# Masks of relation 0 on GpSimd instead of VectorE, with other distances in a written timetable

## The chip, the cores and the metric

The kernel runs on one core of a Trainium2 chip. A core has a matrix engine (TensorE, "PE" in the profile, with its weight loads as "PEld"), VectorE ("DVE"), ScalarE ("ACT"), GpSimd ("POOL") and SyncE ("SP"), which here issues all DMA transfers. The metric is the device time of one execution in microseconds (us), as the median of several runs. TensorE writes its results into PSUM[...].

## The reference, cut to what matters

128 graphs of 128 nodes with 256 features pass through two layers, all in float32.

- Layer 0 is two graph attention steps (GAT): `Wh = h W`, a score for each pair of nodes from two vectors, leaky ReLU, scores where there is no edge replaced by a very low number, softmax, and the weighted sum of `Wh`. Then a residual, a layer norm, a feed-forward (256 to 1024 to 256, ReLU), a residual and a layer norm.
- Layer 1 is an attention of 8 heads with 4 relations, then a layer norm, a feed-forward with GELU, a layer norm. Its core is

```
attn = softmax(q k^T / sqrt(dh))
for r in range(4):
    v_r = src @ Wv[r] + bv[r]
    out += (attn * (adj == r)) @ v_r
```

The change is about `attn * (adj == r)`. The adjacency holds the integers 0 and 1, but the kernel computes all four relations, as the reference does.

## The kernel before, in words

The graphs are worked on in 32 groups of G = 4. Each group goes through five stages, written as Python generators: load, GAT (`gat_block`, with `gat_weighting` called twice), the feed-forward of layer 0 (`feed_forward`), `attention`, and the feed-forward of layer 1. Several groups are in flight at once, one in each stage or two.

The order of the work is set by a timetable. Every `yield TIMES[...]` in a stage says how much later its next piece is due. A heap (`todo`, lines 587 to 613) always takes the piece with the earliest due time, at the same time the earlier stage first. Group g's stages start at 100 g plus -75, -39, 48, 132 and 300, except at the first and last groups, where `EARLY` shifts them. TensorE and SyncE must keep the order in which the pieces are taken (`KEPT`; TensorE from due time 250 on). On VectorE, ScalarE and GpSimd a planner puts the instructions in order by its own estimate of when they are ready. Each engine then works through its list strictly in that order, and waits are semaphores.

The lines that the change and the steps of the prediction touch:

- GAT: L392 computes `wh` and L393 copies it. In `gat_weighting` a row of scores is turned by L366 and sent through DRAM (`zs`, `zsd`), L373 is the leaky ReLU, L374 applies `cap` (made by L387 from the adjacency, `at`), L376 the maximum, L379 the exponential, L381 on GpSimd the division. L400 and L410 are the two weighted sums on TensorE, and L401 copies L400's result.
- Feed-forward: seven products of half size for each unit (L307; a fast matrix scheme), with two units in turn. L313, L314, L320 copy, L321, L322, L325 add on VectorE, L327 and L333 are the activations on ScalarE. The last product of each unit adds to the PSUM tile `chain`, and must come after L325 has read that tile. L350 is the second matrix, L351 the residual. L283 to L286 on GpSimd make the sums of the inputs that the products use.
- Attention: L424 and L430 give q and k, L435 copies the adjacency into PSUM as float32 (`adj`), L444 the scores of one graph (`weights`), L450 the maximum, L454 the exponential, L456 on GpSimd the division, then `turned` transposes the weights (L262 and a round trip through DRAM, `zd`, into `eT`). L470 makes the four masked copies `m` of `eT`, one for each relation, L477 and L478 give `v` for all relations, L489 the weighted sum of all relations and heads (64 instructions for a graph, relation 3 first and 0 last in each half), L493 copies it, L527 applies `Wo`.
- Layer norms: L230 and L231 on VectorE, L233 to L237 on GpSimd, L239 on ScalarE; the gains and offsets that are still to be applied are L245 on GpSimd (`affine`).
- `mm`, the tile for nearly all results of TensorE, has six PSUM buffers; `adj` and `av` have one each.

Of the kernel before, what the change touches and what calls it, by code (L numbers as in the profile page):

```python
# [12 lines left out]
F32 = mybir.dt.float32  # L13
I32 = mybir.dt.int32
AF = mybir.ActivationFunctionType
OP = mybir.AluOpType
# [6 lines left out]
P = 128  # L23
G = 4

TIMES = {
    "sums": 5, "ff unit": 3, "ff2": 4, "ff half": 10, "row": 13, "gat": 16, "wh": 5.5,
    "gat copy": 2, "qk": 4.5, "scores": 5.5, "turn0": 10, "turn1": 5,
    "v0": 5.5, "mask0": 0, "av": 6.5, "v": 3.5, "mask": 3,
    "end": 1, "lead ff0": 26, "lead att": 32, "lead ff1": 32, "affine": 7,  # L30
    "store": 25,
# [26 lines left out]
def graph_layers(ctx: ExitStack, tc: tile.TileContext, a: dict, out: bass.AP):  # L58
# [8 lines left out]
    nc = tc.nc  # L67
    x, xT, adjT = a["x"], a["xT"], a["adjT"]
    NG, N, _, D = x.shape
# [6 lines left out]
    R = a["wv"].shape[1] // D  # L76
    H = 8
# [7 lines left out]
    wk = ctx.enter_context(tc.tile_pool(name="wk", bufs=2))  # L85
# [14 lines left out]
    def load_mask(g):  # L100
        at = ld.tile([P, G, N], I32, name="at")
        nc.sync.dma_start(at, adjT[g])
        return at

    def wload(name, t=None):

        k, m = a[name].shape
        if t is None:
            t = cst.tile([P, k // P, m], F32, name=name)
        nc.sync.dma_start(t, a[name].rearrange("(c p) m -> p c m", p=P))  # L110
        return t
# [11 lines left out]
    m = wload("M", wk.tile([P, DC, MW], F32, name="m_in", tag="wh", bufs=1))  # L123
# [100 lines left out]
    def normalised(y, first=0, n=G):  # L224

        y = y[:, first:first + n]
        mv = sm.tile([P, n, 2], F32, name="mv")
        for b in range(n):
            st = sm.tile([P, 6], F32, name="st")
            nc.vector.bn_stats(st, y[:, b])  # L230
            nc.vector.bn_aggr(mv[:, b], st)  # L231
        rstd = sm.tile([P, n], F32, name="rstd")
        nc.gpsimd.tensor_scalar(rstd, mv[:, :, 1], EPS, None, op0=OP.add)  # L233
        nmr = sm.tile([P, n], F32, name="nmr")
        nc.gpsimd.tensor_scalar(nmr, mv[:, :, 0], -1.0, None, op0=OP.mult)
        nc.gpsimd.tensor_tensor(rstd, rstd, mhalf[:, :n], OP.pow)
        nc.gpsimd.tensor_mul(nmr, nmr, rstd)  # L237
        for b in range(n):
            nc.scalar.activation(y[:, b], y[:, b], AF.Identity, bias=nmr[:, b:b + 1], scale=rstd[:, b:b + 1])  # L239
# [117 lines left out]
    def gat_weighting(wh, c, cap, direct):  # L357

        e = wk.tile([P, G, N], F32, name="e")
        if direct:  # L360
            p = ps.tile([P, G, N], F32, name="mm")
            for b in range(G):
                nc.tensor.transpose(p[:, b], wh[:, b, c + 1:c + 2].to_broadcast([P, N]), ident)
        else:
            z = sm.tile([P, G, Q], F32, name="zs", bufs=2)
            nc.vector.transpose(z, wh[:, :, c + 1:c + 2].to_broadcast([P, G, Q]))  # L366
            s = dr.tile([G, NQ, Q], F32, name="zsd")
            nc.sync.dma_start(s.rearrange("b i t -> i b t"), z[::Q])
            p = e
            nc.sync.dma_start(p, bass.AP(tensor=s.tensor, offset=s.offset, ap=[[0, P], [1, G * N]]))  # L370
        yield TIMES["row"]
        for b in range(G):
            nc.scalar.activation(e[:, b], p[:, b], AF.Prelu, bias=wh[:, b, c:c + 1], alpha=ALPHA)  # L373
        nc.vector.scalar_tensor_tensor(e, cap, BIG, e, op0=OP.subtract, op1=OP.min)  # L374
        nm = sm.tile([P, G], F32, name="nm")
        nc.vector.tensor_reduce(nm, e, AX.X, OP.max, negate=True)  # L376
        s = sm.tile([P, G], F32, name="s")
        for b in range(G):
            nc.scalar.activation(e[:, b], e[:, b], AF.Exp, bias=nm[:, b:b + 1], accum_out=s[:, b:b + 1])  # L379
        nc.vector.reciprocal(s, s)  # L380
        nc.gpsimd.tensor_mul(e, e, per_row(s, N))  # L381
        return e

    def gat_block(direct, tag, g, xt, at):

        cap = wk.tile([P, G, N], F32, name="cap")
        nc.vector.tensor_scalar(cap, at, 0, 2 * BIG, op0=OP.is_gt, op1=OP.mult)  # L387
        wh = wk.tile([P, G, MW], F32, name="wh", tag=tag, bufs=TB if tag == "T" else 1)
        for b in range(G):
            p = ps.tile([P, MW], F32, name="mm")  # L390
            for c in range(DC):
                nc.tensor.matmul(p, xt[:, c, ts(b, N)], wx[:, c], start=c == 0, stop=c == DC - 1)  # L392
            nc.scalar.copy(wh[:, b], p)  # L393
            if b % 2:
                yield TIMES["wh"]
        att = yield from gat_weighting(wh, D + 2, cap, direct)
        yield TIMES["gat"]
        for b in range(G):
            p = ps.tile([P, D + 2], F32, name="mm")
            nc.tensor.matmul(p, att[:, b], wh[:, b, :D + 2], start=True, stop=True)  # L400
            nc.scalar.copy(wh[:, b, :D + 2], p)  # L401
        yield TIMES["gat copy"]
        y = wk.tile([P, G, D], F32, name="tok", bufs=KB)
        nc.sync.dma_start(y, x[g])
        att = yield from gat_weighting(wh, D, cap, direct)
        yield TIMES["gat"]
        for b2_ in range(0, G, 2):
            p = ps.tile([P, 2, D], F32, name="mm")
            for b in (b2_, b2_ + 1):
                nc.tensor.matmul(p[:, b - b2_], att[:, b], wh[:, b, :D], start=True, stop=True)  # L410
            nc.vector.tensor_add(y[:, b2_:b2_ + 2], y[:, b2_:b2_ + 2], p)
        normalised(y)
        return y

    def attention(y, g, first, direct):

        hT = features(y, first or direct)
        at = load_mask(g)
# [14 lines left out]

        adj = ps.tile([P, G, N], F32, name="adj", bufs=1)
        nc.vector.tensor_copy(adj, at)  # L435

        def weights(b):


            scores = [ps.tile([P, DC, 2, N], F32, name="mm") for _ in range(2)]  # L440
            for c in range(DC):
                for h in range(2):
                    rows = ts(h, P // 2)
                    nc.tensor.matmul(scores[h][:, c], qT[rows, c, ts(b, N)], kbd[c][rows, b],  # L444
                                     start=True, stop=True, tile_position=(h * P // 2, 0))
            e = wk.tile([P, H, N], F32, name="e1")
            for h, p in enumerate(scores):
                p = p.rearrange("p c q n -> p (c q) n")
                nm = sm.tile([P, HC], F32, name="nm1")
                nc.vector.tensor_reduce(nm, p, AX.X, OP.max, negate=True)  # L450
                s = sm.tile([P, HC], F32, name="s1")
                eh = e[:, ts(h, HC)]
                for q in range(HC):
                    nc.scalar.activation(eh[:, q], p[:, q], AF.Exp, bias=nm[:, q:q + 1], accum_out=s[:, q:q + 1])  # L454
                nc.vector.reciprocal(s, s)  # L455
                nc.gpsimd.tensor_mul(eh, eh, per_row(s, N))  # L456
            return e

        def turned(e):
            eT = wk.tile([P, H, N], F32, name="eT")  # L460
            transposed(e, eT, direct, e)
            return eT

        def by_relation(b, eT, ms, parts):


            ab = adj[:, b][:, None, :].to_broadcast([P, H, N])
            for r in parts:
                m = ms[r] = wk.tile([P, H, N], F32, name="m", bufs=R)
                nc.vector.scalar_tensor_tensor(m, ab, r, eT, op0=OP.is_equal, op1=OP.mult)  # L470

        def values(b):
            v = wk.tile([P, R, D], F32, name="v")
            for r in range(0, R, 2):
                p = ps.tile([P, 2, D], F32, name="mm")
                for f in range(DC):
                    nc.tensor.matmul(p, hT[:, b, f], wv[:, f, r:r + 2], start=f == 0, stop=f == DC - 1)  # L477
                nc.vector.tensor_add(v[:, r:r + 2].rearrange("p r d -> p (r d)"),  # L478
                                     p.rearrange("p r d -> p (r d)"), bv[:, r * D:(r + 2) * D])
            return v  # L480
# [20 lines left out]
        eT = [turned(es[0])]  # L501
        yield TIMES["turn1"]
        eT.append(turned(es[1]))
        yield TIMES["v0"]
        PARTS = range(R)
        v, ms = values(0), {}
        for k in range(0, 8, 2):
            by_relation(0, eT[0], ms, PARTS[k // 2:k // 2 + 1])
            yield TIMES["mask0"]
        for b in range(G):  # L510
# [8 lines left out]
            for k in range(0, 8, 2):  # L519
                if b + 1 < G:  # L520
                    by_relation(b + 1, eT[b + 1], ms, PARTS[k // 2:k // 2 + 1])
                if k == 2 and b + 1 < G:
# [30 lines left out]
    def stage_gat(g):  # L553
        x0[g] = yield from gat_block(g < 2, "T" if g == 1 else "wh", g, *loads.pop(g))
# [109 lines left out]
```

## Time and profile before

| | |
|---|---|
| median of 3 runs | 3208.48 us (3208.29 to 3210.35) |
| span of the profiled execution | 3208.9 us |
| TensorE busy | 3124.8 us, 97% |
| VectorE busy | 2019.9 us, 63% |
| ScalarE busy | 1688.2 us, 53% |
| GpSimd busy | 1377.3 us, 43% |
| masks, L470 on VectorE | 512 operations, 598.8 us |
| DMA | 320.8 MB, 43.5% of 16 engines |

A group of instructions in the profile is named by line, engine and operation, with what it writes and reads. "Idle before" is the time that the engine stood still just ahead of an instruction, with the instruction on another engine that released it. In the timeline, consecutive instructions of one kind are one row, with their number. A float32 matmul of the program is two matmul instructions in the trace.

### The profile page before, as it was taken

Reading aid. Unit: us, or ns where it says so; the run is one execution under the profiler, and the core shown is the slowest. Engines: PE = TensorE matmul, PEld = TensorE weight load, DVE = VectorE, ACT = ScalarE, POOL = GpSimd, SP = SyncE. Lnnn points to the kernel's source line nnn. Section 1 sums busy time; section 2 is a strip of 40 time slices with the busy share of each in tenths; the row PEclk is TensorE's granted clock in tenths of the full one; section 3 lists DMA queues with packets and bytes.
Section 4 is the critical chain, followed back from the end, with each engine's and each line's share of the span. In section 5 each row is a group of like instructions: output and inputs, shape, how many; then the busy total and the mean of one; then the engine's idle time right before and its main releaser. Section 6 shows DMA issues by size and latency. Waiting matters only on the chain.

```text
span 3208.9 us, 55180 instructions
## 1 busy us (share of the span) xinstructions
PE 3124.8 (97%) x20160; PEld 2377.2 (74%) x20160; DVE 2019.9 (63%) x3654; ACT 1688.2 (53%) x5063; POOL 1377.3 (43%) x1734
## 2 busy tenths in 40 slices
PE   6989999999999999999999999999999999999998
PEld 5756777777777777777777777777777777777666
DVE  3566566666566666576666576666576666576563
ACT  4435555555555555555555555555555555555443
POOL 2324345345345344345344345344345344345342
PEclk8999999999999999999999999999999999999999
DMA  4244454444454444454444454444454444454310
GB/s 156 66 105 96 102 119 102 107 99 100 102 120 104 105 98 101 101 120 104 105 100 98 101 120 104 104 99 99 102 120 104 104 99 99 102 120 92 73 34 14
DMA packets 1156399, 320.82 MB, mean 100 GB/s; under 512 B 902944, under 2 KB 1126688, under 8 KB 1156000
## 3 DMA queue, kind: packets, MB, share of 16 engines
q1 hardware_dynamic: 1156128, 317.29, 43.5%
q8 instruction: 160, 2.62, 0.3%
q14 instruction: 111, 0.91, 0.1%
HBM read 187.58 MB, written 129.62 MB: 99 GB/s over the span
## 4 chain that ended last, share of the span: by engine, by line
PE 58%; DVE 4%; DMA 1%; issue 0%; ACT 0%; POOL 0%; SPq 0%; ACTq 0%; POOLq 0%; DVEq 0%
PE mm L350 18%; PE mm L307 15%; PE mm L477 7%; PE av L489 5%; DVE m L470 3%; PE mm L444 3%; PE mm L527 2%; PE mm L430 2%; PE mm L424 2%; PE mm L392 2%; PE mm L400 1%; PE mm L410 1%; DVE fT L325 0%; DVE fT L322 0%; DMA eT<-zd 0%
## 5 line engine op out<-in xcount | busy, mean ns | idle before, releaser
L470 DVE SCALAR_TENSOR_TENSOR m<-adj,eT 128x1024 f32<-128x1024 f32 x512 | 598.8, 1213 | 242.5 <-DMA eT<-zd 176.9
L245 POOL TENSOR_TENSOR tok<-tok,ln_rows 128x512 f32<-128x512 f32 (+1 forms) x636 | 668.6, 1059 | 42.2 <-PE mm L256 14.8
L456 POOL TENSOR_TENSOR e<-e,s 128x512 f32<-128x512 f32 x256 | 266.1, 1040 | 660.9 <-DVE s L455 648.9
L454 ACT ACTIVATE e<-mm,nm 128x128 f32<-128x128 f32 x1024 | 359.8, 374 | 199.7 <-DVE nm L450 178.0
L477 PE MATMUL mm<-wv,T 128*128 128x512 f32 x1024 | 464.2, 596 | 0.0
L350 PE MATMUL mm<-wf,fT 128*128 128x256 f32 x2048 | 456.9, 381 | 0.0
L350 PE MATMUL mm<-w,fT 128*128 128x256 f32 x2048 | 455.5, 381 | 1.1 <-DVE v L478 1.1
L350 PEld LDWEIGHTS mm<-w,fT 128*128 128x128 f32 x2048 | 386.6, 190 | 75.5 <-issue 23.8
L350 PEld LDWEIGHTS mm<-wf,fT 128*128 128x128 f32 x2048 | 386.4, 190 | 63.3 <-ACT wh L401 8.9
L239 ACT ACTIVATE tok<-tok,nmr,rstd 128x256 f32<-128x256 f32 x512 | 269.2, 594 | 137.7 <-POOL nmr L237 125.1
L477 PEld LDWEIGHTS mm<-wv,T 128*128 128x128 f32 x1024 | 191.5, 190 | 199.6 <-issue 189.3
L351 DVE TENSOR_TENSOR tok<-tok,mm 128x512 f32<-128x512 f32 x128 | 87.8, 686 | 299.4 <-PE mm L350 295.4
L381 POOL TENSOR_TENSOR e<-e,s 128x512 f32<-128x512 f32 x64 | 66.9, 1046 | 475.3 <-DVE s L380 381.1
L489 PE MATMUL av<-m,v 128*32 128x128 f32 x8192 | 256.2, 277 | 8.1 <-DVE v L478 4.2
L489 PEld LDWEIGHTS av<-m,v 128*32 128x32 f32 x8192 | 219.8, 111 | 54.1 <-issue 42.2
L283 POOL TENSOR_TENSOR t<-T 128x256 f32<-128x256 f32 x64 | 46.7, 729 | 483.6 <-DMA T<-zd 483.6
L454 ACT ACTIVATION_READ_ACCUMULATOR e<-mm,nm 128x1 f32 x1024 | 218.8, 214 | 0.0
L450 DVE TENSOR_REDUCE nm<-mm 128x4 f32<-128x512 f32 x256 | 162.9, 676 | 64.0 <-PE mm L444 64.0
L478 DVE TENSOR_TENSOR v<-mm,bv 128x512 f32<-128x512 f32 x256 | 167.5, 684 | 46.9 <-PE mm L477 46.9
L307 PE MATMUL mm<-T,w 128*128 128x256 f32 x768 | 196.5, 385 | 0.2 <-ACT T L260 0.2
L307 PE MATMUL mm<-T,wf 128*128 128x256 f32 x768 | 192.6, 380 | 0.0
L373 ACT ACTIVATE e<-e,wh 128x128 f32<-128x128 f32 x240 | 77.3, 408 | 210.2 <-DMA e<-zsd 210.2
(123 smaller groups left out, 5090.1 us busy)
## 6 DMA issues: line engine op xcount, KB each, us to landing
zd<-e SPq DMA_DIRECT2D x496, 128.0 KB, 3.1
eT<-zd SPq DMA_DIRECT2D x124, 512.0 KB, 4.0
zd<-T SPq DMA_DIRECT2D x364, 128.0 KB, 4.0
T<-zd SPq DMA_DIRECT2D x91, 512.0 KB, 4.0
xt<-in_xT_dram SPq DMA_DIRECT2D x32, 512.0 KB
at<-in_adjT_dram SPq DMA_DIRECT2D x64, 256.0 KB, 6.2
tok<-in_x_dram SPq DMA_DIRECT2D x32, 512.0 KB
out_dram<-tok SPq DMA_DIRECT2D x31, 512.0 KB, 7.5
```

The costliest lines, as they stand in the source:

```text
L239: nc.scalar.activation(y[:, b], y[:, b], AF.Identity, bias=nmr[:, b:b + 1], scale=rstd[:, b:b + 1])
L245: engine.tensor_tensor(y[:, b:b + n], y[:, b:b + n], v[:, None, :].to_broadcast([P, n, D]), op)
L307: nc.tensor.matmul(p[:, i], win[k][:, ts(f0 + i, P)], hs[k], start=first and i == 0, stop=True, skip_group_check=True)
L350: nc.tensor.matmul(p[:, b - b2_], fT[f][:, ts(b, N)], wout[:, f], start=n == 0, stop=n == FC - 1)
L444: nc.tensor.matmul(scores[h][:, c], qT[rows, c, ts(b, N)], kbd[c][rows, b], start=True, stop=True, tile_position=(h * P // 2, 0))
L450: nc.vector.tensor_reduce(nm, p, AX.X, OP.max, negate=True)
L454: nc.scalar.activation(eh[:, q], p[:, q], AF.Exp, bias=nm[:, q:q + 1], accum_out=s[:, q:q + 1])
L456: nc.gpsimd.tensor_mul(eh, eh, per_row(s, N))
L470: nc.vector.scalar_tensor_tensor(m, ab, r, eT, op0=OP.is_equal, op1=OP.mult)
L477: nc.tensor.matmul(p, hT[:, b, f], wv[:, f, r:r + 2], start=f == 0, stop=f == DC - 1)
L478: nc.vector.tensor_add(v[:, r:r + 2].rearrange("p r d -> p (r d)"), p.rearrange("p r d -> p (r d)"), bv[:, r * D:(r + 2) * D])
L489: last = nc.tensor.matmul(po[ts(q, DH), c], v[:, r, c * P + q * DH:c * P + (q + 1) * DH], ms[r][:, q // 2 * HC + c * 2 + q % 2], start=r = ...
```

## The change

```diff
 TIMES = {
-    "sums": 5, "ff unit": 3, "ff2": 4, "ff half": 10, "row": 13, "gat": 16, "wh": 5.5,
-    "gat copy": 2, "qk": 4.5, "scores": 5.5, "turn0": 10, "turn1": 5,
+    "sums": 6, "ff unit": 3, "ff2": 5, "ff half": 10, "row": 13, "gat": 18, "wh": 7.5,
+    "gat copy": 3, "qk": 4.5, "scores": 6, "turn0": 10, "turn1": 5,
...
-        cap = wk.tile([P, G, N], F32, name="cap")
+        cap = wk.tile([P, G, N], F32, name="cap", bufs=1)
...
         nc.vector.tensor_copy(adj, at)
+        zero = wk.tile([P, G, N], F32, name="zero", bufs=1)
+        nc.vector.tensor_scalar(zero, at, 0, None, op0=OP.is_equal)
...
-                nc.vector.scalar_tensor_tensor(m, ab, r, eT, op0=OP.is_equal, op1=OP.mult)
+                if r == 0:
+                    nc.gpsimd.tensor_mul(m, eT, zero[:, b][:, None, :].to_broadcast([P, H, N]))
+                else:
+                    nc.vector.scalar_tensor_tensor(m, ab, r, eT, op0=OP.is_equal, op1=OP.mult)
...
-        PARTS = range(R)
+        PARTS = (0, 3, 2, 1)
```

Of the four masked copies of each graph's weights, the one of relation 0 is now made by GpSimd: VectorE writes once for each group a tile `zero` with 1 where the adjacency is 0 and 0 elsewhere, and GpSimd multiplies. It is meant to take work from VectorE and give it to the less busy GpSimd. The copies are asked for in the order 0, 3, 2, 1, so that GpSimd's is asked for first and VectorE makes them in the order in which L489 reads them. `cap` has one buffer instead of two, which makes room in SBUF for `zero`. The timetable gives GAT, the feed-forwards and the scores other distances, so that the stages of neighbouring groups are interleaved in another order on TensorE.

## The prediction

> **What bounds the kernel now.** I read four views in this order: the busy totals, the busy time by stretch, the waits of TensorE alone, and then the timeline of one period, first TensorE, then VectorE and ScalarE beside it.
>
> ```profile
> PE 3124.8 (97%) x20160; PEld 2377.2 (74%) x20160; DVE 2019.9 (63%) x3654; ACT 1688.2 (53%) x5063; POOL 1377.3 (43%) x1734
> ```
> TensorE is busy for all but 84 us; no other engine comes near. By stretch (columns: span, then busy time of PE, PEld, DVE, ACT, POOL, granted clock, DMA):
> ```profile
> 300.00:2900.00 2600.00, 2583.78 (x16853) 1971.10 (x16853) 1688.55 (x3051) 1420.87 (x4271) 1163.04 (x1459) 1.00 0.47 105
> 0.00:100.00 100.00, 75.72 (x313) 61.51 (x314) 33.35 (x85) 41.59 (x121) 26.50 (x39) 0.86 0.43 146
> 200.00:300.00 100.00, 82.33 (x581) 57.10 (x580) 56.70 (x96) 48.28 (x166) 31.85 (x41) 0.90 0.44 98
> 2900.00:3209.00 309.00, 283.03 (x1834) 213.88 (x1832) 172.10 (x309) 135.67 (x378) 125.47 (x160) 0.96 0.24 54
> ```
> The 84 us are 24.3 at the start, 17.7 at 200 to 300 us, 26.0 at the end, and only 2600 - 2583.8 = 16.2 us in the 27 periods between. The waits of TensorE in those 2600 us are one line:
> ```profile
> PE mm L307 <- DVE fT L325: 16.2, 27, 1.1
> ```
> So the steady part has exactly one recurring hole: 27 times, 0.6 us each. One period shows it. TensorE:
> ```profile
> 1566.64 3.60 PE L477 MATMUL mm<-wv,T 128*128 128x512 f32 x8
> 1570.81 1.97 PE L307 MATMUL mm<-t,wf 128*128 128x256 f32 x8 [0.57 <-DVE fT L325]
> 1572.61 1.90 PE L400 MATMUL mm<-wh,e 128*128 128x258 f32 x8
> 1574.44 1.95 PE L489 MATMUL av<-m,v 128*32 128x128 f32 x64
> 1576.33 1.15 PE L444 MATMUL mm<-kbd,T 64*128 64x256 f32 x8
> ```
> and VectorE in the same microseconds:
> ```profile
> 1564.86 4.61 DVE L470 SCALAR_TENSOR_TENSOR m<-adj,eT 128x1024 f32<-128x1024 f32 x4
> 1569.38 0.68 DVE L322 TENSOR_TENSOR fT<-fT,mm 128x512 f32<-128x512 f32 x1
> 1569.98 1.28 DVE L325 TENSOR_TENSOR fT<-fT,mm 128x512 f32<-128x512 f32 x2
> 1571.17 1.28 DVE L478 TENSOR_TENSOR v<-mm,bv 128x512 f32<-128x512 f32 x2
> ```
> The four masks of graph 0 stand ahead of L322 and L325 on VectorE. The first L325 ends at about 1570.6, and TensorE's last product of the feed-forward unit (L307) goes on at 1570.81. The same product comes back every 96.24 us (1570.81 and 2918.18 are 14 periods apart). The chain of waits says the same: "DVE m L470 x3" of 3.48 us is its only long piece off TensorE in each period. **At most 16.2 us, 0.5%, can be won in the steady part**; the rest is start, ramp and end.
>
> **What the Trainium skill says.** (1) "GPSIMD Engine Reference", 3.1 (Elementwise): a two-input elementwise operation reads both inputs through one port, about 2.6 cycles an element, about half of VectorE's speed. The trace agrees: L245 goes from 738 ns at 256 columns to 1276 ns at 512, 2.1 ns a column, against 1213 ns for 1024 columns of L470. (2) "SBUF — State Buffer", Who interferes with whom: a VectorE operation with two SBUF inputs, or in a two-port mode, and a GpSimd operation that reads SBUF exclude each other for a whole instruction. L374 (cap and e, both in SBUF) takes 693 ns in the median and up to 1192; the 1.18 us one at 1556.22 ends its delay as GpSimd's L245 ends at 1556.85. L470 reads adj from PSUM and isn't lengthened (4.61 us for four with GpSimd busy). (3) "TensorE: Matmul & The Clock Gate", Part 1: a TensorE that idles for some microseconds comes back at half clock. Seen in the ramp: after 5.29 us of waiting, L400 x8 takes 3.81 us instead of 1.90; after 0.57 us nothing happens.
>
> **The change, part by part.**
> *Masks.* VectorE loses 128 of 512 L470 operations: 598.8 / 4 = 150 us. It gains 32 of "zero", the same shape and types as cap (L387, 412 ns): 13 us. VectorE 2020 -> 1883 us.
> GpSimd gains 128 products of 1024 columns. Not in the trace; bounds from rows: twice L456 (1040 ns at 512, one input repeated along the row) = 2.08 us, twice L245 (1276, two full streams) = 2.55. L245's line carried on: 1276 + 512 x 2.1 = 2.35 us, and I take this since zero, like ln_rows, is read in full. 128 x 2.35 = 301 us; GpSimd 1377 -> 1678 us, 52%. Not a bound in total.
> *Where it lies.* For graphs 1, 2 and 3 GpSimd has idle stretches where the masks are due (1573.7 to 1580.1, 1598 to 1600, 1617.7 to 1635.2 us), and VectorE's masks end 12, 8 and 9 us ahead of their L489. For graph 0 it is tight: GpSimd is nearly full from 1560.2 to 1573.7, and 2.35 us go in there. L489 reads relation 3 first and 0 last, 24 of 64 matmuls (0.7 us) later, which helps.
> *The gain.* With three masks ahead of them, L322 and both L325 end 1.15 us earlier: the first L325 at about 1569.5, while TensorE is in L477 until 1570.1. The hole of 0.57 closes. VectorE's L478 (v) then ends at about 1571.4, before the next user at 1571.8.
> *Order of r.* m has four buffers, written in turn. The first mask now waits for relation 0's buffer on GpSimd, and VectorE's first (relation 3) needs a buffer that L489 drops at 5/8 of its work. Earlier than before; no cost.
> *Timetable.* TensorE follows the due times. Adding the distances for one period (mod 100): L400 moves from 1 to 7, L489 of graph 0 from 1 to 1.5, L477 from 7.5 to 8, the first L350 from 7 to 9, L410 from 32 to 41. The order L400, L489, L444, L350, L477 becomes **L489, L444, L400, L477, L350**; L410 goes behind L527 and the first L307 of the second feed-forward. In real time L400 is about 2.4 us later, L410 2.6 us (two groups, 0.86 + 1.73). Behind L410 hang normalisation, transposes, DMA and L283, which ended at 1635.2 + 2.9 for a first use at 1651.7: 13 us of room, so this costs nothing. Between L400 and L410 the chain through zs and e ends at 1593.9 for 1602.2: 8 us of room for up to 3 us of delay. The stage starts and the period stay, so no work is added on TensorE.
> *The risk in it: PSUM.* mm has six buffers. At L400 the two chain buffers of the units (freed by ScalarE's L333), two of L444 (freed by the exponentials) and four of L400 come together with two of L477: ten, in 6 us, where before the 7 us of L350 stood between. Before, ScalarE was just in time:
> ```profile
> 1573.18 1.69 ACT L333 ACTIVATE fT<-fT,col 128x256 f32<-128x256 f32 x4
> 1574.77 1.52 ACT L333 ACTIVATE fT<-mm,col 128x256 f32<-128x256 f32 x4
> 1576.19 1.17 ACT L401 COPY wh<-mm 128x258 f32<-128x258 f32 x4
> ```
> L333 ends at 1576.2 and L444 starts at 1576.33. Now L477 wants a third buffer back at about 1576.5. If ScalarE, which should be done with L333 at 1575.4 because L325 is earlier, takes a copy of L400 first: free at 1575.9, no wait. If it takes four exponentials first (1.36 us) after L493 (0.4): 1577.2 to 1577.4, a wait of 0.7 to 0.9 us. I take no wait, since the first L400 product is ready 0.43 us after L444 and the exponentials must wait for L450 (0.68 us) besides; both ends stay in the range.
> *cap with one buffer.* In the steady part cap is read last at 1588.9 and written at 1618.1: free. At the start two groups run together: L374 at 29.6 and 30.9, then 42.5 and 44.1. Group 1 must now wait for 42.5 + 0.7, so its L400 comes some 10 us later, L410 some 4 to 8. TensorE waits there anyhow (5.2 and 4.4 us) and has the feed-forward of group 0 from 60 us: 0 to 4 us, I take 1.
> *Ramp at 205 to 255 us.* L400 used to fill a hole ahead of L489, which waited for its masks (3.9 us); now L489 comes first and TensorE idles through to about 225. Its end is one mask (1.15 us) earlier, L400 later. By the second feed-forward's start I get 254 against 253.9: -2 to +3, I take 0.5.
> *Sum.* 3208.5 - 15.5 (27 x 0.57) + 1.5 = **3194 us**.
>
> **Rivals.**
> A, as above, 52%: 3194, -0.45%.
> B, the hole moves: TensorE waits 0.4 to 0.9 us for a PSUM buffer ahead of L477, or for v ahead of L489 (0.4 us of room), instead of 0.57. For it: six buffers, and VectorE and ScalarE in order. Against: ScalarE's work can be ordered round it. 27 x (-0.2 to +0.3) + 1.5: 3204 to 3219, middle 3211. 27%.
> C, slower: GpSimd's mask at graph 0 pushes L236 and L237, which ScalarE's L239 waits for (1569.96, released by L237), and L333 stands behind L239 on ScalarE; or L489 waits for the mask itself. Up to 2.35 us late, say 1.5 us a period: 27 x (1.5 - 0.57) + 1.5: 3235. For it: GpSimd's full 13 us. Against: affine steps (L245) that nobody waits for can go behind. 13%.
> D, A and a better ramp (up to 8 of its 17.7 us): 3186. 8%.
>
> **Numbers.** Faster by over 6.4 us: A, D less a little for a poor start = 0.58. Within: the lower half of B and some of A = 0.17. Slower: the rest of B and C = 0.25. Range 3184 to 3224: below it little of D, above it most of C.
>
> **What would show it.** Right: the wait of L307 on L325 gone from 300 to 2900 us, TensorE's busy time there near 2599 of 2600, period 95.7 us; GpSimd's products of 1024 columns at 2.1 to 2.6 us; L470 x384. B: a new line of waits of TensorE, L477 or L400 on ScalarE (L454, L401, L333), or L489 on L478. C: L489 on GpSimd's m, or L239's wait on L237 longer. Wrong altogether if the period differs with no wait beside it.

## The result, and the profile after

**Slower: 3266.19 us in the median (3256.9 to 3272.14), against 3209.41 before (four runs of each); ratio 1.0174 (95% interval 1.0149 to 1.02).** The forecast was 3194, its range 3184 to 3224. The profiled execution has a span of 3255.1 us; it is the fastest of the four, so the profile shows 46 of the 57 us.

The busy totals of the kernel after, and its busy time by stretch (span, then PE, PEld, DVE, ACT, POOL, granted clock, DMA):

```profile
PE 3134.4 (96%) x20160; PEld 2368.7 (73%) x20160; DVE 1889.5 (58%) x3558; ACT 1679.1 (52%) x5063; POOL 1672.9 (51%) x1862
```
```profile
200.00:300.00 100.00, 81.29 (x575) 53.89 (x573) 53.08 (x91) 45.84 (x153) 38.95 (x42) 0.90 0.43 95
300.00:2900.00 2600.00, 2553.00 (x16550) 1935.30 (x16550) 1550.88 (x2922) 1386.98 (x4203) 1389.44 (x1540) 1.00 0.46 103
```

From 0 to 100 us TensorE is busy for 73.37 us, from 100 to 200 for 96.76, from 2900 us to the end for 329.96 of 355.1. So the difference of the two spans can be added up. TensorE's idle time from 300 to 2900 us goes from 16.2 to 47.0 us (+30.8), before 300 us from 42.0 to 48.6 (+6.5), at the end it falls by 0.7; its busy time grows by 9.6 (3134.4 - 3124.8). Together 46.2 us. So the loss is mainly in the steady part, where TensorE now waits in two new places (the waits of TensorE of the kernel after, 300 to 2900 us: microseconds in total, times, longest):

```profile
PE mm L482 <- ACT e L456: 25.5, 27, 0.9
PE mm L400 <- ACT fT L333: 20.5, 27, 1.4
```

The old line, L307 on L325, is gone from this stretch. Line numbers below `zero` are a few higher than before: L475 makes VectorE's masks (was L470), L473 GpSimd's, L482 and L483 give v (L477, L478), L494 is the weighted sum (L489), L446 the scores (L444), L452 and L456 the maximum and exponential (L450, L454), L498 the copy (L493), L532 the product with `Wo` (L527).

One period of TensorE after, at the place shown before:

```profile
1498.50 1.96 PE L307 MATMUL mm<-t,wf 128*128 128x256 f32 x8
1500.39 1.95 PE L494 MATMUL av<-m,v 128*32 128x128 f32 x64
1502.28 1.14 PE L446 MATMUL mm<-kbd,T 64*128 64x256 f32 x8
1503.34 1.57 PE L400 MATMUL mm<-wh,e 128*128 128x258 f32 x6
1505.54 0.70 PE L400 MATMUL mm<-wh,e 128*128 128x258 f32 x2 [0.63 <-ACT fT L333]
1507.19 3.70 PE L482 MATMUL mm<-wv,T 128*128 128x512 f32 x8 [0.95 <-ACT e L456]
```

The order is the forecast one: L494, L446, L400, L482. L307 has no wait ahead of it, as the plan had it. But then the fourth product of L400 finds no PSUM buffer, and neither does L482. This period is 97.79 us (L494 comes at 1500.39 and again at 1598.18) against 96.24. Of the 1.55 us more, 1.1 are idle time (1.70 a period from the two waits, 0.60 before) and 0.45 busy time: L400 in two pieces takes 1.57 + 0.70 instead of 1.90, L482 3.70 instead of 3.60.

VectorE in the same microseconds, with three masks ahead of L322 and L325:

```profile
1493.62 3.47 DVE L475 SCALAR_TENSOR_TENSOR m<-adj,eT 128x1024 f32<-128x1024 f32 x3
...
1497.70 1.25 DVE L325 TENSOR_TENSOR fT<-fT,mm 128x512 f32<-128x512 f32 x2
1498.87 1.27 DVE L483 TENSOR_TENSOR v<-mm,bv 128x512 f32<-128x512 f32 x2
```

The first L325 ends at about 1498.3, ahead of L307 at 1498.50. That half of the plan worked. ScalarE is what is late:

```profile
1497.19 2.08 ACT L239 ACTIVATE tok<-tok,nmr,rstd 128x256 f32<-128x256 f32 x4 [3.11 <-POOL nmr L237]
...
1500.40 1.69 ACT L333 ACTIVATE fT<-fT,col 128x256 f32<-128x256 f32 x4
...
1502.70 2.06 ACT L239 ACTIVATE tok<-tok,nmr,rstd 128x256 f32<-128x256 f32 x4
1504.67 0.82 ACT L333 ACTIVATE fT<-mm,col 128x256 f32<-128x256 f32 x2
```

It stood still for 3.11 us at the layer norm L239, released by L237 on GpSimd. L333, which frees the two `chain` buffers, stands behind this L239 in ScalarE's list, and the L239 of a second layer norm (2.06 us) stands between its halves. It is done at 1505.49, that is 7.0 us after TensorE began the last products of the unit (L307 at 1498.50); before, it was 5.5 us (1576.29 against 1570.81). TensorE had done the first three products of L400 at 1504.91, 6.4 us after that start, and had to wait for the fourth. And L237 is late because of GpSimd:

```profile
1491.94 1.04 POOL L236 TENSOR_TENSOR rstd<-rstd,mhalf 128x4 f32<-128x4 f32 x1
1492.95 2.36 POOL L473 TENSOR_TENSOR m<-eT,zero 128x1024 f32<-128x1024 f32 x1
1495.26 0.73 POOL L245 TENSOR_TENSOR tok<-tok,ln_rows 128x256 f32<-128x256 f32 x1
1495.95 1.05 POOL L381 TENSOR_TENSOR e<-e,s 128x512 f32<-128x512 f32 x1
1496.95 0.21 POOL L237 TENSOR_TENSOR nmr<-nmr,rstd 128x4 f32<-128x4 f32 x1
```

The mask of graph 0 stands between L236 and L237, two instructions of one layer norm that depend on each other, with an affine step and a division behind it. L237 could have run at 1493.0 and ran at 1496.95.

### The profile page after: what moved, and what is told of

Same layout as the page of the kernel before. It is cut to its first block, busy times and chain, and to the rows that moved or that the text cites. A ratio compares the mean times of both kernels' runs of the same rounds, so it can differ in the third digit from the quotient of the medians.

```text
span 3255.1 us, 55075 instructions
## 1 busy us (share of the span) xinstructions
PE 3134.4 (96%) x20160; PEld 2368.7 (73%) x20160; DVE 1889.5 (58%) x3558; ACT 1679.1 (52%) x5063; POOL 1672.9 (51%) x1862
## 5 line engine op out<-in xcount | busy, mean ns | idle before, releaser
L475 DVE SCALAR_TENSOR_TENSOR m<-adj,eT 128x1024 f32<-128x1024 f32 x384 | 450.7, 1208 | 180.1 <-DMA eT<-zd 178.2
L473 POOL TENSOR_TENSOR m<-eT,zero 128x1024 f32<-128x1024 f32 x128 | 302.3, 2362 | 476.6 <-DMA eT<-zd 275.0
L482 PE MATMUL mm<-wv,T 128*128 128x512 f32 x1024 | 469.1, 601 | 26.8 <-ACT e L456 26.8
L456 ACT ACTIVATE e<-mm,nm 128x128 f32<-128x128 f32 x1024 | 360.7, 378 | 172.9 <-DVE nm L452 150.4
L350 PEld LDWEIGHTS mm<-wf,fT 128*128 128x128 f32 x2048 | 389.9, 190 | 66.4 <-issue 16.2
L482 PEld LDWEIGHTS mm<-wv,T 128*128 128x128 f32 x1024 | 190.1, 191 | 237.5 <-issue 186.8
L239 ACT ACTIVATE tok<-tok,nmr,rstd 128x256 f32<-128x256 f32 x512 | 265.9, 599 | 176.9 <-POOL nmr L237 176.9
L494 PE MATMUL av<-m,v 128*32 128x128 f32 x8192 | 254.7, 276 | 14.3 <-DVE m L475 10.5
L494 PEld LDWEIGHTS av<-m,v 128*32 128x32 f32 x8192 | 217.5, 111 | 62.1 <-issue 43.6
L452 DVE TENSOR_REDUCE nm<-mm 128x4 f32<-128x512 f32 x256 | 163.3, 678 | 126.5 <-PE mm L446 126.5
L456 ACT ACTIVATION_READ_ACCUMULATOR e<-mm,nm 128x1 f32 x1024 | 222.6, 217 | 0.0
L483 DVE TENSOR_TENSOR v<-mm,bv 128x512 f32<-128x512 f32 x256 | 170.3, 684 | 62.6 <-PE mm L482 61.4
L307 PE MATMUL mm<-T,w 128*128 128x256 f32 x768 | 196.7, 386 | 0.2 <-ACT T L260 0.2
L307 PE MATMUL mm<-T,wf 128*128 128x256 f32 x768 | 192.2, 380 | 0.0
L457 DVE RECIPROCAL s<-s 128x4 f32<-128x4 f32 x256 | 45.2, 177 | 246.6 <-ACT e L456 246.5
```

The costliest lines, as they stand in the source:

```text
L307: nc.tensor.matmul(p[:, i], win[k][:, ts(f0 + i, P)], hs[k], start=first and i == 0, stop=True, skip_group_check=True)
L350: nc.tensor.matmul(p[:, b - b2_], fT[f][:, ts(b, N)], wout[:, f], start=n == 0, stop=n == FC - 1)
L473: nc.gpsimd.tensor_mul(m, eT, zero[:, b][:, None, :].to_broadcast([P, H, N]))
L494: last = nc.tensor.matmul(po[ts(q, DH), c], v[:, r, c * P + q * DH:c * P + (q + 1) * DH], ms[r][:, q // 2 * HC + c * 2 + q % 2], start=r = ...
```

## Experiments

Two theories stood at the start. **P**: the timetable's new order makes TensorE ask for more PSUM buffers in a few microseconds than come back. **G**: the GpSimd mask makes ScalarE late by way of L237. Both are read off the profile above, and a profile doesn't tell which of two things is needed. The ratios below are against further runs of the kernel before, whose medians lie between 3207.99 and 3211.5 us.

**1 and 2: each half of the change alone.** The first keeps GpSimd's masks and takes the old distances:

```diff
-    "sums": 6, "ff unit": 3, "ff2": 5, "ff half": 10, "row": 13, "gat": 18, "wh": 7.5,
-    "gat copy": 3, "qk": 4.5, "scores": 6, "turn0": 10, "turn1": 5,
+    "sums": 5, "ff unit": 3, "ff2": 4, "ff half": 10, "row": 13, "gat": 16, "wh": 5.5,
+    "gat copy": 2, "qk": 4.5, "scores": 5.5, "turn0": 10, "turn1": 5,
```

> The changed kernel with the old distances of the timetable; the masks of relation 0 stay on GpSimd, cap has one buffer. Theory P (the new order of TensorE brings L400 and L482 together and runs out of PSUM buffers): the waits of L400 on L333 (0.63 us a period) and of L482 on L456 (0.94) are gone, and so is the old hole of 0.57, since only three masks stand ahead of L325: period near 95.8 us, time 3190 to 3202. Theory G (the mask on GpSimd delays L237, so L239 and the L333 behind it): ScalarE is as late as in the changed kernel, L444 waits for the buffers that L333 frees, 0.5 to 1.5 us a period: 3215 to 3245.

Measured: 3339.76 us, ratio 1.0405 (1.0388 to 1.0422). Neither number was near. There is no wait on L333 or L456, but others (waits of TensorE of this kernel, 300 to 2900 us, and VectorE's list in one period):

```profile
PE mm L424 <- DVE v L483: 59.2, 25, 3.5
```
```profile
1582.29 0.68 DVE L483 TENSOR_TENSOR v<-mm,bv 128x512 f32<-128x512 f32 x1
1590.68 1.23 DVE L475 SCALAR_TENSOR_TENSOR m<-adj,eT 128x1024 f32<-128x1024 f32 x1 [7.71 <-DMA eT<-zd]
1591.82 0.68 DVE L483 TENSOR_TENSOR v<-mm,bv 128x512 f32<-128x512 f32 x1
```

A mask that waits 7.71 us for `eT` stands between the two additions of v, and the second one holds a PSUM buffer that L424 wants, and L532 too (24.9 us more).

The second experiment is the kernel before with the new distances only (the reverse of the diff above, on the kernel before).

> The kernel before with only the new distances of the timetable; all masks on VectorE, cap with two buffers. Theory P: L400 and L482 wait for buffers as in the changed kernel, and the old hole on L325 may be there too: 3245 to 3275. Theory G: without the mask on GpSimd, L239 and L333 are on time, the waits are 0.3 us or less: 3205 to 3222.

Measured: 3241.7 us, 1.0096 (1.0081 to 1.0111). No wait on L333 or L456 either: the new order doesn't run out of PSUM here. (L307 comes late in this kernel, which gives ScalarE time; experiment 6 has the order without that.) But the old hole grew. VectorE and TensorE in one period of this kernel (its lines are those of before):

```profile
1585.30 1.21 DVE L470 SCALAR_TENSOR_TENSOR m<-adj,eT 128x1024 f32<-128x1024 f32 x1
...
1586.52 1.24 DVE L325 TENSOR_TENSOR fT<-fT,mm 128x512 f32<-128x512 f32 x2
```
```profile
1587.31 1.97 PE L307 MATMUL mm<-t,wf 128*128 128x256 f32 x8 [1.15 <-POOL nmr L235]
```

The fourth mask stands right ahead of L325, and L307 loses 1.15 us a period at this point instead of 0.57, and 0.5 more at a second one. The profile puts the wait down to L235 on GpSimd, which ended last, at 1587.22; but L307 doesn't read its result, and the first L325, which L307 does need, ended at about 1587.1. What follows from both: the new distances need one mask less ahead of L325, and GpSimd's masks need the new distances. The new distances alone cost 31 us, GpSimd's masks alone 129. In these two kernels neither half by itself makes the two waits of the changed kernel.

**3: the first weighting back in its place, all else as changed.** L400 is due at 1 again, as before the change; L410 stays at its new time.

```diff
-        yield TIMES["gat"]
+        yield TIMES["gat"] - 6
...
-        yield TIMES["gat copy"]
+        yield TIMES["gat copy"] + 6
```

> The changed kernel with one piece moved back in the timetable: L400 is due 6 earlier, ahead of L494 of graph 0 as in the kernel before, and L410 stays where the change puts it. Theory P: L400 has its four buffers before L446 asks for two, and L350 no longer follows L482: one of the two waits, that of L400 on L333, goes, and L482, right behind L446, may have a wait of up to 0.5 us: 3200 to 3225. Theory G: L239 and L333 as late as before, a wait of L446 on L333 takes the place of that of L400: 3235 to 3260.

Measured: **3200.29 us, 0.9971 (0.9962 to 0.9981): faster than the kernel before**, at the lower edge of P's range and far from G's. TensorE in one period of this kernel:

```profile
1570.64 1.90 PE L400 MATMUL mm<-wh,e 128*128 128x258 f32 x8
1572.38 1.03 PE L307 MATMUL mm<-t,wf 128*128 128x256 f32 x4
1573.34 1.95 PE L494 MATMUL av<-m,v 128*32 128x128 f32 x64
```

L400 now stands between the two groups of the last L307, ahead of L494 and of L446 and L482 that follow, and its copies (L401, from 1575.08 on) give buffers back about when L446 (1575.22) and L482 (1576.56) ask: L446 waits for a copy 3 times, 1.0 us in all. TensorE is busy for 2597.3 of the 2600 us. ScalarE still waits 3.11 us for L237, for the same GpSimd mask between L236 and L237. So G's cause is there in full, and costs next to nothing: it needs the late L400 to hurt.

**4: the copies of L400 on VectorE.** This takes the copies out of ScalarE's list and leaves TensorE's order.

```diff
-            nc.scalar.copy(wh[:, b, :D + 2], p)
+            nc.vector.tensor_copy(wh[:, b, :D + 2], p)
```

> The changed kernel with the four copies of L400's result (L401) made by VectorE instead of ScalarE, so that their buffers come free without waiting in ScalarE's list. Theory P: the wait of L482 on ScalarE's exponentials (0.94 us a period) goes, since it can take a buffer of L400; the wait of L400's last product on L333 (0.63) stays: 3225 to 3242. Theory G: L482's wait is due to ScalarE being late as a whole and goes as well, and with 1.2 us less on ScalarE so does some of the other: 3215 to 3235. If neither time nor waits move, the buffers are not what L482 waits for.

Measured: 3223.31 us, 1.004 (1.0025 to 1.0055). The time lies just below P's range and inside G's, but the waits are those that P named. The wait of L482 is gone and that of L400 on L333 stays (20.0 us in 27 times): they are two shortages, the second made by the order exponentials before copies on ScalarE, the first by L333 itself.

**5: the old distances once more, with VectorE's masks behind v.** If the mask between the two additions is all that is wrong in the first experiment, this mends it. (`after` puts an instruction behind another in its engine's list, without a wait; `newest()` is the instruction just issued.)

```diff
+                if k == 2 and b + 1 < G:
+                    v = values(b + 1)
+                    added = newest().name
                 if b + 1 < G:
                     by_relation(b + 1, eT[b + 1], ms, PARTS[k // 2:k // 2 + 1])
-                if k == 2 and b + 1 < G:
-                    v = values(b + 1)
+                    if k and b + 1 > 1:
+                        after(newest(), added)
```

> The kernel of old distances with masks on GpSimd (3340 us), with one order more: VectorE's masks of graphs 2 and 3 may not stand ahead of the additions that make v of the same graph (L483 there, L490 here). Theory L (VectorE's list: a mask that waits for eT holds back the addition behind it, which holds the PSUM buffer that L424 and L532 want): the waits of L424 (2.4 us a period) and L532 (1.0) on v go, and the period falls from 100 to 96 to 96.5: 3200 to 3225. Theory G (GpSimd's masks make everything behind them late, eT too): the waits move to other instructions, mostly L494, and the time stays over 3300.

Measured: 3306.68 us, 1.0303 (1.0286 to 1.032). Both waits on v are gone, but only 33 of 129 us with them; a new wait comes up at the start of the second feed-forward (lines stand 7 higher here: L314 is L307, L320 is L313, L480 is L473, L244 is L237, L246 is L239). L314 waits for L320 26 times, 62.0 us in all. GpSimd and ScalarE of this kernel:

```profile
1547.81 2.35 POOL L480 TENSOR_TENSOR m<-eT,zero 128x1024 f32<-128x1024 f32 x1 [1.95 <-DMA eT<-zd]
...
1555.51 0.21 POOL L244 TENSOR_TENSOR nmr<-nmr,rstd 128x4 f32<-128x4 f32 x1
```
```profile
1555.75 2.08 ACT L246 ACTIVATE tok<-tok,nmr,rstd 128x256 f32<-128x256 f32 x4 [5.33 <-POOL nmr L244]
```

It is the pattern of the changed kernel at another place: a GpSimd mask ahead of the scalars of a layer norm (here it even waits for its own input first), ScalarE 5.33 us at L246, and the copies that free PSUM behind it (the first L320 begins at 1557.73).

**6: only graph 0's mask back on VectorE**, behind v there; 96 of 128 masks stay on GpSimd, the distances and TensorE's order are those of the change.

```diff
-                if r == 0:
+                if r == 0 and b:
...
+                    if r == 0:
+                        after(newest(), added)
...
+        added = newest().name
...
-            by_relation(0, eT[0], ms, PARTS[k // 2:k // 2 + 1])
+            by_relation(0, eT[0], ms, (3 - k // 2,))
```

> The changed kernel, with the mask of relation 0 of graph 0 alone back on VectorE, where it comes last of the four and behind the additions for v, so that neither GpSimd nor the adds L325 are held up by it. The order of TensorE stays as the change has it. Theory G (the mask on GpSimd between L236 and L237 makes L239 and then L333 late): ScalarE's wait of 3.1 us for the norm's scalars falls under 1 us, the wait of L400 on L333 (0.63 us a period) goes and that of L482 on the exponentials falls to 0 to 0.4: 3205 to 3222. Theory P (the order of TensorE alone runs out of PSUM buffers): both waits stay, 3245 to 3265.

Measured: 3206.4 us, 0.9987 (0.9981 to 0.9994). Both waits are gone (2596.0 of 2600 us busy), with L400 as late as in the change. ScalarE in one period (lines stand 7 higher: L246 is L239, L340 is L333, L314 is L307):

```profile
1475.29 2.07 ACT L246 ACTIVATE tok<-tok,nmr,rstd 128x256 f32<-128x256 f32 x4 [0.80 <-POOL nmr L244]
...
1480.97 2.06 ACT L246 ACTIVATE tok<-tok,nmr,rstd 128x256 f32<-128x256 f32 x4
...
1482.94 1.53 ACT L340 ACTIVATE fT<-mm,col 128x256 f32<-128x256 f32 x4
```

The second layer norm stands within L333's work here too, but ScalarE stood still for 0.80 us at the first one instead of 3.11, and L333 is done 5.6 us after L307 began (1484.47 against 1478.91), not 7.0. That is in time for the fourth product of L400. So the loss can be taken away at either end.

**7: the third experiment's distances, all masks on VectorE.** This asks whether GpSimd's masks earn anything where nothing else stands in the way. The edit is the two lines of experiment 3 on the kernel of experiment 2.

> The timetable that gave 3200 us with masks on GpSimd (new distances, L400 back in its old place), but with all masks on VectorE as in the kernel before. If GpSimd's masks are what closed the hole of L307 on L325, it is here again with 0.6 to 1.2 us a period: 3212 to 3240. If the timetable closed it, the time is 3192 to 3203.

Measured: 3245.14 us, 1.0109 (1.0095 to 1.0122), 5 us above the range, with the hole of experiment 2 again (L307 waits 32.0 and 13.1 us in all, 27 times each). Against experiment 3, in these distances the GpSimd masks are worth 45 us. How much of that needs GpSimd isn't shown: experiment 6 had graph 0's fourth mask on VectorE behind v, without the hole, and all masks on VectorE in that order weren't tried.

**8: experiment 3, with group 1's `cap` in a slot of its own**, so that the two groups at the start don't share one buffer.

```diff
-        cap = wk.tile([P, G, N], F32, name="cap", bufs=1)
+        cap = wk.tile([P, G, N], F32, name="cap", tag="e1" if g == 1 else "cap", bufs=2 if g == 1 else 1)
```

> The kernel of 3200 us (changed kernel with L400 back in its place), where cap of group 1 lies in memory that is unused at the start (the slots of the attention weights), so that group 1 no longer waits for group 0; all other groups share one cap as before. If the single cap costs time at the start: TensorE's idle time in the first 200 us falls from 30.9 to about 24.5 us and the time by 4 to 7 us, to 3193 to 3197. If it doesn't, 3199 to 3202, and the 30.9 us come from the masks on GpSimd in the ramp.

Measured: 3200.66 us, 0.9968 (0.9955 to 0.998), as experiment 3. TensorE idles 26.1 us in the first 200 us instead of 30.9, but the time doesn't follow: the profiled span is 2.1 us shorter, the median 0.4 us longer. So the single buffer costs TensorE 4.8 us of idle time at the start, and no gain in the median shows when that is taken away.

**9: all masks on GpSimd, the one of graph 0 ordered behind the scalars.** In experiment 6 GpSimd also had less work. Here it has all of it, and only the order differs (`scaled` is the last L237 issued):

```diff
+                    if b == 0 and g > 1:
+                        after(newest(), scaled[0])
```

> The changed kernel with all relation-0 masks left on GpSimd; only the mask of each group's graph 0 is ordered behind the scalars (L237) of the two layer norms that GpSimd works on at that time. Order theory (the mask's place between L236 and L237, not GpSimd's work, makes ScalarE late): ScalarE's wait of 3.11 us at L239 falls to about 0.8, both PSUM waits (L400 on L333, L482 on L456) go, 3200 to 3212. Rival W (GpSimd has no room there: the mask is only moved late, and the weighted sum L494 waits for it): PSUM waits gone, a new wait of L494 on m of L473 of 0.5 to 1.5 us a period, 3215 to 3240. Rival L (GpSimd's load as such): waits as in the changed kernel, 3250 to 3270.

Measured: 3245.06 us, 1.0104 (1.0089 to 1.012). That is above the range of the order theory and 5 us above rival W's. W's wait, that of the weighted sum, is there, but not for W's cause. The largest wait of TensorE (lines stand 10 to 12 higher: L506 is L494, L494 is L482, L495 is L483, L466 is L456, L487 is L475):

```profile
PE av L506 <- DVE v L495: 36.0, 27, 1.3
```
```profile
1491.39 3.48 DVE L487 SCALAR_TENSOR_TENSOR m<-adj,eT 128x1024 f32<-128x1024 f32 x3
...
1494.79 0.68 DVE L495 TENSOR_TENSOR v<-mm,bv 128x512 f32<-128x512 f32 x1
```

The wait on L333 is gone, that of L482 on the exponentials is down from 0.95 to 0.38 us. The new one isn't on GpSimd's mask, which was ready at 1493.8; it is on v: the planner now put three masks between v's two additions, the second ended at 1495.47, and the weighted sum began at 1495.52, 1.33 us late.

**10: experiments 3 and 9 together.**

> The last kernel's order on GpSimd, with the first weighting back at its due time as in the third experiment. If either repair alone already removes all steady waits, both together add nothing: 3196 to 3204, 2597 of 2600 us busy. If ScalarE's wait still costs something outside the steady part (ramp or end), 3185 to 3195. If the mask comes too late for L494, 3205 to 3230.

Measured: 3207.81 us, 0.9992 (0.9983 to 1.0). A miss: about 7 us slower than experiment 3, in the third range but not for its reason. With the scalars ready early, ScalarE takes both layer norms in one go (L239, eight in 4.03 us) ahead of six of L333's eight operations, and L400 waits for L333 again, 0.5 us in each of 27 periods. In experiment 3, with the scalars late, the second layer norm came behind four of the eight.

**11: experiment 9, with v's additions behind the masks.**

```diff
+                if masked:
+                    after(newest(), masked)
...
-        v, ms = values(0), {}
+        ms = {}
+        by_relation(0, eT[0], ms, PARTS)
+        v = values(0, newest().name)
...
-            by_relation(0, eT[0], ms, PARTS[k // 2:k // 2 + 1])
```

> The kernel of the ninth experiment, with both additions of v for graph 0 ordered behind the three VectorE masks of that graph; before, the masks stood between the two. If the 1.33 us that L494 lost a period is only this order on VectorE: the additions end at about 1494.3 instead of 1495.4, the wait falls to about 0.3, the 0.38 of L482 on the exponentials stays: 3210 to 3222. If it is GpSimd's mask that L494 really waits for, or if another hole takes its place: 3235 to 3250.

Measured: 3212.94 us, 1.0012 (1.0003 to 1.002), within what was expected. The weighted sum's wait falls from 1.33 to 0.21 us (5.7 us in 27 times), and the 0.38 on the exponentials stays.

So the change as it stands, with all 128 masks on GpSimd and its own distances, loses some 52 of its 57 us when the lists of GpSimd and VectorE are put in another order. The amount of work that was moved wasn't the cost; the places that it took were.

## Why the prediction was wrong, point by point

- *What bounds the kernel, and what can be won.* Right: one hole of 0.57 us a period, 16 us in all. Experiment 3 is the changed kernel nearly without waits, and is 10 us faster than before. (27 x 0.57 is 15.4, not 15.5; nothing hangs on it.)
- *Cost of the masks.* Right in every term: 302.3 us on GpSimd for 301 estimated, 2362 ns each for 2.35 us; 384 masks left on VectorE, which is busy for 1889.5 us for 1883; GpSimd at 51%. The two statements of the Trainium skill behind it hold: GpSimd needs twice VectorE's time for the same columns (2362 against 1208 ns, "GPSIMD Engine Reference", 3.1), and L475, which reads `adj` from PSUM, isn't lengthened by a GpSimd that works beside it (1208 ns after, 1213 before; "SBUF — State Buffer", Who interferes with whom). Nor did more work on GpSimd make L374, which reads both inputs from SBUF, longer: 908 ns in the mean before, 737 after.
- *The gain.* Right: L325 ends at about 1498.3, ahead of its user, and the wait is gone.
- *The new order on TensorE.* Right, instruction for instruction.
- *"The risk in it: PSUM", where the step failed.* The text counted ten tiles for six buffers and named both ends of the shortage, and then wrote "I take no wait", because ScalarE "should be done with L333 at 1575.4 because L325 is earlier". L333 doesn't follow L325 alone. It stands behind L239 in ScalarE's list, and L239 waits for L237. In the forecast's times L307's last products begin at 1570.24 (1570.81 without the hole), so L333 was to be done 5.2 us after that; measured were 7.0. Of the 1.8 us that were missing, 1.4 are the late layer norm, since experiment 6, with the same order on TensorE and the scalars on time, needs 5.6. There "no wait" comes true. The waits were 0.63 for L400, which the sum left out though the signs of B name it, and 0.95 for L482, for which it had bounds of 0.7 to 0.9.
- *The mask of graph 0 on GpSimd.* "For graph 0 it is tight" was seen, but the sum let "2.35 us go in there" at no cost. That the mask "pushes L236 and L237" is rival C word for word, with 13%. B, the PSUM buffers, had 27%. They were handled as two different outcomes. They are one chain: C's cause makes B's effect. Experiment 6 takes away the first and experiment 3 the second, and either way all is well, so neither alone would have cost this time (the late L400 alone costs up to 0.38 us a period, as experiment 11 shows). With "say 1.5 us a period", which was a guess, C's size was close (1.7 us of waits), but it left out the 0.45 us that TensorE's work itself takes longer.
- *cap with one buffer.* 1 us, 0 to 4: within bounds. It costs 4.8 us of idle time at the start (experiment 8) and nothing that shows in the time.
- *Ramp.* "-2 to +3" for 205 to 255 us: TensorE idles 1.0 us more from 200 to 300. From 100 to 200 it idles 3.15 us more. About half of that is `cap`'s, since experiment 8 idles 1.65 us there and experiment 3 3.34; no step had named the rest.

The profile of the changed kernel shows 46 of the 57 us; how the other executions come to up to 15 us more than the profiled one wasn't traced. Open as well is why the planner's lists come out so much worse with GpSimd's masks in the old distances; experiments 1 and 5 show a place each, not the reason.

## What to carry to other kernels

When work moves to an engine that has time to spare, don't ask for its share of busy time, but what the moved piece will stand in front of in that engine's list: here 2.36 us between two short, dependent instructions of a layer norm reached TensorE by way of ScalarE. When two risks are found, ask whether one feeds the other before giving each a chance of its own: a late ScalarE and a tight PSUM made waits of 0 to 10 us apart and of 46 us together. And a change of several parts that are tuned to each other can't be judged by its parts: half of this one costs 31 us, the other half 129, both together 57, and both together with one piece of TensorE's work moved back gain 10.

## What was unexpected

A wait on TensorE seems to cost more than its own length. With holes of 0.63 and 0.95 us, L400 and L482 took 0.47 us longer in a period than before (2.27 for 1.90, 3.70 for 3.60). Some of that is the order: behind the scores L400 takes 2.01 us without any wait (experiments 2, 6, 9 and 11). Against experiment 6, which has the same order and no waits, 0.26 and 0.10 us are left, though the granted clock stayed at 1.00. The ends of matmuls are modelled in the trace, so this may be a matter of its records.

A list that looked better wasn't: with the scalars early (experiment 10) the time was about 7 us longer than with ScalarE standing still for 3.11 us in each period (experiment 3).
